# Loads of running sums behind their units' weights, running sums later, delta rule a block later

## The chip, the core and the metric

The kernel runs on one core of a Trainium2 chip. The core has five engines that work side by side, each through its own queue in order: PE (TensorE, matrix products), DVE (VectorE), ACT (ScalarE, functions and copies), POOL (GpSimd) and SP (SyncE), whose queue issues most of the transfers. The metric is the device time of one execution in microseconds (us); lower is better. Of several timed runs the median counts. One further execution was recorded by the hardware profiler, and all statements about single instructions come from it.

## What is computed

All data is float32. The input is `x`, 16 sequences of 128 tokens with 256 features. Three parts follow each other:

```python
x = x + delta_rule(attention(x, cond_1))        # attention and gated delta rule
x = x + quantized_ffn(lora_ffn(x, itok_B_0_7))  # two feed-forward parts
```

The attention has 16 heads of 16 features, a causal mask, and a factor per sequence on the scores. Its output feeds the gated delta rule, of which the part around this change is

```python
g = -exp(A_log) * softplus(h @ W_a + dt_bias)      # logarithms of the decays, 32 heads
g = cumsum(g within chunks of 64 tokens)           # the running sums
decay = tril(exp(g[:, None] - g[None, :]))
A = tril(-(k_beta @ k.T) * decay, -1);  T = inverse(I - A)
u = T @ v_beta;  w = T @ (k_beta * exp(g))
```

Keys, queries and values come from `h @ W_qkv`, a causal convolution over four tokens and a SiLU; keys and queries are normalised. The outputs of the chunks are normalised, gated and projected, and added to `x`. The feed-forward parts are not touched by the change.

## The kernel before

The 16 sequences are cut into four groups of four (512 tokens). There are two streams of work, which the kernel weaves together in one program order.

**The attention** (`attention()`) works in blocks: one sequence and half of the heads, so 32 blocks, eight to a group. A block multiplies keys with queries (L243 on PE), masks (L248, DVE), takes the largest (L253, DVE), subtracts it (L256, POOL), takes the exponent (L259, ACT), sums and inverts (L263, L264, DVE), multiplies to shares (L267, POOL), turns them (L274 on PE, copied by L275 on ACT), weighs the values (L282, PE) and picks the halves that belong together (L289 on ACT, L290 on DVE). Three buffers `sc` hold the scores of blocks in flight. A group's output steps are two products with the output weights (L306), the logarithms (`logs`, L310 to L334: product L316, functions on ACT, `gd` on DVE at L332) and `running`. This last forms the running sums by three products with triangular matrices (L339, L341), copies them on DVE (L343, L346) and stores them to DRAM as `sums` (L344).

Each step has a due time, in blocks: block number plus an offset inside the block. A group's output steps are due 2.15, 2.45, 3.0 and 3.6 after the group's last block has started its own slot, so that `running` is due 0.6 blocks behind `logs`.

**The delta rule** works in units: one key head (two value heads) and one group, so 64 units, in groups of 16 heads. Slot `n` of the main loop (L857) issues the steps of several units at once: the keys of unit `n`, the decays of unit `n - 1`, the inverse for batches of four units (five and six slots late), values, merging and outputs from seven slots late. Inside a slot each step has a time between 0 and 24.

A unit's keys are two projections (L455, PE), convolutions (L464 ACT, L466 DVE, three shifts each), SiLU (L483), squares (L487), norms (L493 PE, L495 DVE), and the factors on POOL (L500 to L507). Its decays start from the running sums: `load_sums(n)` (L428 to L434) loads for a pair of units, `n` and `n + 1`, the sums as the tile `aT` with two transfers of 512 KB each, repeated on all 128 partitions. Five such buffers exist, so that ten units fit. `fades(n)` then subtracts offsets (L443, POOL), masks (L444, POOL) and takes the exponent of the pair (L448, ACT). A weight follows (L522, POOL), and two sets of products of keys with keys and queries (L530 PE, L534 DVE). The diagonal blocks go through small transfers (L543) to one tile for four units, from which the inverse is formed (L557 to L638, mostly DVE). `load_qk(u)` (L392 to L396) loads the unit's key and query weights `w_qk` in two transfers; there are two buffers.

**How the two are woven.** Attention steps due before `ALONE` run first, alone. The others are dealt out over the slots, `PACE` blocks to a slot:

```python
ALONE, PACE = 11.2, 3.9
...
now = [a for a in ahead if a[0] < ALONE + PACE * (n + 1)]
plan([f for _, _, f in now], [24 * ((t - ALONE) / PACE - n) for t, _, _ in now])
```

With these values the attention is done in slot 6, and the other buffers of the delta rule are opened in slot 7.

**What sets the order on an engine.** The kernel is written in a framework that records the instructions in program order with their dependencies, then orders each engine's queue itself: earlier program order has priority, but an instruction that its model of the machine takes to be ready may pass one that is not. So a transfer whose buffer is free can be moved far ahead of its place in the program. This holds for `load_sums`, which the main loop calls at the end of every odd slot and which at first finds all five buffers free. `tc.issue_after(ins)` adds an order to this: what is issued inside it on the engine of `ins` stays behind `ins` in the queue. It adds no wait for completion.

Of the kernel before, what the change touches and what calls it, by code (L numbers as in the profile page):

```python
# [15 lines left out]
P = 128  # L16
# [14 lines left out]
KEY = NK * P  # L31
# [25 lines left out]
def tile_adaln_attn_ffn(  # L57
# [8 lines left out]
    nc = tc.nc  # L66
# [81 lines left out]
    GB = GS * ND  # L148

    def attention():  # L150
# [144 lines left out]
        def output(g):  # L295


            d = {}

            def product(e):  # L300
                if e == 0:
                    hTs[g] = keep.tile([P, ND, GT], F32, name="hT", tag="hT", bufs=2) if g < 2 else \
                        p1.tile([P, ND, GT], F32, name="hT_out", tag="hT_out", bufs=1)
                ps = ps_b.tile([P, GT], F32, name="ps_h", tag="b")
                for c in range(ND):
                    T.matmul(ps, lhsT=wo_sb[:, c, e * P : (e + 1) * P], rhs=grp[g]["oT"][:, c, :],  # L306
                             start=c == 0, stop=c == ND - 1)
                A.copy(hTs[g][:, e, :], ps)

            def logs():  # L310
                if g > 1:
                    nc.sync.dma_start(out=h_dram[g], in_=hTs[g])
                ps = ps_b.tile([P, GS, 2 * NV], F32, name="ps_ba", tag="b")
                for j in range(GS):
                    for c in range(ND):
                        T.matmul(ps[:, j, :], lhsT=hTs[g][:, c, j * S : (j + 1) * S], rhs=wba[:, c, :],  # L316
                                 start=c == 0, stop=c == ND - 1)
                a = p1.tile([P, GS, NV], F32, name="a", tag="ga", bufs=1)
                e = p1.tile([P, GS, NV], F32, name="ea", tag="ge", bufs=1)

                A.activation(e, ps[:, :, 0:NV], AF.Exp, scale=-1.0)
                V.tensor_tensor(a, ps[:, :, NV:], dtb[:, None, :].to_broadcast([P, GS, NV]), ALU.add)
                V.tensor_scalar(e, e, 1.0, None, ALU.add)
                V.reciprocal(beta[:, :, g * GS : (g + 1) * GS, :].rearrange("p k b h -> p b k h"),
                             e.rearrange("p b (k h) -> p b k h", h=2))

                V.scalar_tensor_tensor(out=e, in0=a, scalar=-1.0, in1=a, op0=ALU.mult, op1=ALU.max)
                A.activation(e, e, AF.Exp, scale=-1.0)
                A.activation(e, e, AF.Ln, bias=one)
                V.scalar_tensor_tensor(out=a, in0=a, scalar=0.0, in1=e, op0=ALU.max, op1=ALU.add)  # L330
                gd = d["gd"] = p1.tile([P, NK, GS, 2], F32, name="gd", tag="gd", bufs=1)
                V.tensor_tensor(gd.rearrange("p k b h -> p b k h"), a.rearrange("p b (k h) -> p b k h", h=2),  # L332
                                nega.rearrange("p (k h) -> p k h", h=2)[:, None, :, :].to_broadcast([P, GS, NK, 2]),
                                ALU.mult)  # L334

            def running():
                gd = d["gd"].rearrange("p k b h -> p (k b h)")
                ps = ps_b.tile([P, 3, NK * NP], F32, name="ps_sums", tag="b")
                T.matmul(ps[:, 0, :], lhsT=gd, rhs=tri, start=True, stop=True)  # L339
                for i, w in enumerate((tri, tri_2)):  # L340
                    T.matmul(ps[:, 1 + i, :], lhsT=w, rhs=gd, start=True, stop=True)  # L341
                rows = p1.tile([P, S], F32, name="rows", tag="ge", bufs=1)
                V.tensor_copy(rows, ps[:, 0, :])  # L343
                nc.sync.dma_start(out=sums[g], in_=rows)  # L344
                for i in range(2):
                    V.tensor_copy(off[:, :, g * GS : (g + 1) * GS, :, i].rearrange("p k b h -> p k (b h)"),  # L346
                                  ps[:, 1 + i, :].rearrange("p (k q) -> p k q", k=NK))

            return [lambda: product(0), lambda: product(1), logs, running]
# [3 lines left out]
        def plan(t0, fs, times):  # L353
            steps.extend((t0 + t, len(steps) + i, f) for i, (t, f) in enumerate(zip(times, fs, strict=True)))

        for g in range(NG):
            t0 = GB * g
            plan(t0, project(g), [-2, -1.8, -1, -0.8, -0.6, -0.4] if g == 0 else [-6.55, -5.55, -4.55, -3.55, -2.85, -1.85])
            for i in range(GS):
                for e in range(ND):  # L360
                    plan(t0 + ND * i + e, block(g, i, e), [0, 0.15, 0.3, 0.45, 0.5, 1.0, 1.05, 1.45, 2.2, 2.45, 2.6, 2.8])
            plan(t0 + GB, output(g), [2.15, 2.45, 3.0, 3.6])
        return sorted(steps, key=lambda t: t[:2])


# [23 lines left out]
    qkv = w_qkv.rearrange("(c p) f -> p c f", p=P)  # L389
    w_qk, w_v, w_gate, w_o, x_in, sum_of, un, batch = {}, {}, {}, {}, {}, {}, {}, {}  # L390

    def load_qk(u):  # L392
        kh, g = u
        w = w_qk[u] = w2.tile([P, ND, 2, P], F32, name="w_qk", tag="wqk")
        nc.sync.dma_start(out=w[:, :, 0, :], in_=qkv[:, :, kh * P : (kh + 1) * P])
        nc.sync.dma_start(out=w[:, :, 1, :], in_=qkv[:, :, KEY + kh * P : KEY + (kh + 1) * P])  # L396

    def load_v(u):
        kh, g = u
# [24 lines left out]
    def load_h(g):  # L424
        hTs[g] = keep.tile([P, ND, GT], F32, name="hT", tag="hT", bufs=2)
        nc.sync.dma_start(out=hTs[g], in_=h_dram[g])

    def load_sums(n):  # L428

        t = sum_of[n] = pc.tile([P, 2, NP, S], F32, name="aT", tag="aT", bufs=5)  # L430
        for i in range(2):
            kh, g = units[n + i]
            nc.sync.dma_start(out=t[:, i].rearrange("p q t -> p (q t)"),
                              in_=sums[g][kh * NP : (kh + 1) * NP].rearrange("q t -> (q t)").partition_broadcast(P))  # L434
# [410 lines left out]
    MERGE, OUT, LAST = 7, 8, 10  # L845
    N = len(units)

    ALONE, PACE = 11.2, 3.9
    load_qk(units[0])
    ahead = attention()  # L850
    while ahead and ahead[0][0] < ALONE:
        ahead.pop(0)[2]()
    for n in range(N + LAST):
        at = lambda lag: units[n - lag] if 0 <= n - lag < N else None
        slot = []

        def plan(steps, times):
            slot.extend((t, len(slot) + i, f) for i, (t, f) in enumerate(zip(times, steps, strict=True)))  # L860

        def spread(steps, t0=0.0, t1=24.0):
            plan(steps, [t0 + (t1 - t0) * (i + 0.5) / len(steps) for i in range(len(steps))])

        now = [a for a in ahead if a[0] < ALONE + PACE * (n + 1)]
        plan([f for _, _, f in now], [24 * ((t - ALONE) / PACE - n) for t, _, _ in now])
        del ahead[: len(now)]
        if n == 0:
            plan([lambda: load_sums(0)], [5])
        if n == MERGE:  # L870
            assert not ahead
            st_1.close()
            open_late()
            load_v(at(MERGE))
        if n + 1 < N:
            load_qk(units[n + 1])
        if at(MERGE - 1) and n >= MERGE:
            load_v(at(MERGE - 1))
        if at(OUT - 1):
            load_z(at(OUT - 1))  # L880
        if at(LAST - 1):
            load_o(at(LAST - 1))
        if n % NK == OUT + 1 and 1 <= n // NK < NG - 1:
            load_h(n // NK + 1)
        if at(MERGE) or at(MERGE + 1):
            steps = mergers(at(MERGE), at(MERGE + 1))
            plan(steps, [0, 0, 8, 14] if at(MERGE) else [14])
        if at(1):
            plan(decays(at(1)), [0, 4.5, 9, 10])
        if at(0):  # L890
            plan(keys(at(0)), [2, 5, 6.0, 10, 12.0, 14, 19])
        if n % 2 == 0 and n < N:
            plan(fades(n), [8, 12, 19])
        if at(MERGE):
            plan(values(at(MERGE)), [5.5, 8.5, 9, 15.5, 18, 23])
        if at(OUT):
            plan(outputs(at(OUT)), [13, 20, 16, 17, 19, 22, 23.5])
        if at(LAST):
            plan(finish_unit(at(LAST)), [0, 8, 14, 14])
        if at(NU + 1) and (n - NU - 1) % NU == 0:  # L900
            first, second = inverse((n - NU - 1) // NU)
            spread(first)
        elif at(NU + 2) and (n - NU - 2) % NU == 0:
            plan(second, [0, 1, 4, 6, 7, 13, 15, 17])
        for _, _, f in sorted(slot, key=lambda t: t[:2]):
            f()
        if n % 2 and n + 1 < N:
            load_sums(n + 1)
        if n == N + 2:
            ffn_loads()  # L910
    late["stack"].close()
# [236 lines left out]
```

## Time and profile before

| | |
|---|---|
| Median of 3 runs | 2430.25 us (2428.03 to 2436.76) |
| The profiled execution | 2431.28 us |
| Its span (first to last instruction) | 2429.6 us |
| PE busy in the span | 2200.7 us, 91% |
| DVE busy | 1548.1 us, 64% |
| ACT busy | 1361.7 us, 56% |
| POOL busy | 1145.9 us, 47% |
| Mean granted TensorE clock | 0.954 |

The profile gives busy time per engine, also in slices and in freely chosen stretches. In a stretch's line stand its bounds and length, then the busy microseconds of PE, of PE's weight loads, of DVE, ACT and POOL, each with its number of instructions, then the granted TensorE clock, the share of the DMA engines and GB/s. A timeline lists instructions by start and length; in brackets stands idle time of the engine just ahead, and which engine and tile ended it. The view of waits adds such idle times up: total, how many, the longest. Tiles are written as output and inputs, `aT<-sums` for example.

### The profile page before, as it was taken

The numbers are of one execution on the slowest core, as the hardware profiler recorded it, in microseconds if no ns is written. First come the engines' busy times: TensorE is split into PE (matmuls) and PEld (weight loads), VectorE is DVE, ScalarE is ACT, GpSimd is POOL, SyncE is SP. The second block draws the span as 40 slices with busy tenths as digits, with TensorE's granted clock in tenths as the row PEclk, the third lists the DMA queues.
The fourth block names the chain that finished last, engine by engine and source line by source line (L and its number), as shares of the span: only waits on it lengthen the run. The fifth ranks groups of instructions, "written<-read, shape, count | busy, mean of one in ns | idle before, by whom it ended". The sixth has DMA issues, their size and how long they took to land. (4 is left out here: it accounts for less than half of the span.)

```text
span 2429.6 us, 41939 instructions
## 1 busy us (share of the span) xinstructions
PE 2200.7 (91%) x16248; PEld 1450.2 (60%) x16248; DVE 1548.1 (64%) x2102; ACT 1361.7 (56%) x3008; POOL 1145.9 (47%) x833
## 2 busy tenths in 40 slices
PE   7868759989999998989999998989999898999999
PEld 3433336766667666766666666766677686344445
DVE  4657878687776968687777868687876831311111
ACT  3566536766666666766666666766666574111110
POOL 4585535465555656465555656465556413700000
PEclk9889879999999999999999999999999999999999
DMA  1200022222222322322223222222322323000000
GB/s 56 91 17 15 24 56 76 70 66 71 68 66 77 104 72 64 75 68 68 68 80 86 82 73 64 77 66 68 85 69 80 89 52 123 26 0 20 9 0 18
DMA packets 289910, 148.37 MB, mean 61 GB/s; under 512 B 184241, under 2 KB 278193, under 8 KB 289713
## 3 DMA queue, kind: packets, MB, share of 16 engines
q1 hardware_dynamic: 287792, 141.44, 21.1%
q0 software_dynamic: 1344, 4.20, 0.5%
q8 instruction: 131, 2.15, 0.4%
q14 instruction: 67, 0.54, 0.1%
q10 hardware_dynamic: 576, 0.05, 0.0%
HBM read 119.13 MB, written 5.51 MB: 51 GB/s over the span
## 5 line engine op out<-in xcount | busy, mean ns | idle before, releaser
L466 DVE SCALAR_TENSOR_TENSOR cv<-ps_in,cw,cv 128x500 f32<-128x500 f32 (+2 forms) x768 | 540.2, 735 | 88.8 <-ACT cv L464 84.2
L455 PE MATMUL ps_in<-hT,w_v 128*128 128x512 f32 x512 | 281.5, 679 | 6.8 <-DVE z L770 4.6
L464 ACT ACTIVATE cv<-ps_in,cw 128x512 f32<-128x512 f32 x256 | 174.5, 682 | 182.7 <-PE ps_in L455 182.0
L770 DVE TENSOR_TENSOR z<-ps_ot,z 128x512 f32<-128x512 f32 x128 | 87.9, 687 | 289.9 <-ACT sq L768 289.9
L455 PE MATMUL ps_in<-hT,w_qk 128*128 128x512 f32 x512 | 251.3, 613 | 7.1 <-DVE z L770 6.2
L743 PE MATMUL ps_z<-w_gate,hT 128*128 128x256 f32 x1024 | 242.3, 379 | 1.7 <-DVE z L770 1.7
L800 PE MATMUL ps_out<-wo_head,zT 128*128 128x256 f32 x1024 | 238.8, 386 | 1.0 <-ACT zT L792 1.0
L500 POOL TENSOR_SCALAR nn<-turned 128x4 f32<-128x4 f32 x64 | 15.6, 244 | 419.4 <-DVE turned L495 316.8
L800 PEld LDWEIGHTS ps_out<-wo_head,zT 128*128 128x128 f32 x1024 | 189.0, 190 | 38.0 <-issue 10.7
L743 PEld LDWEIGHTS ps_z<-w_gate,hT 128*128 128x128 f32 x1024 | 189.4, 190 | 27.7 <-DVE z L770 2.6
L455 PEld LDWEIGHTS ps_in<-hT,w_v 128*128 128x128 f32 x512 | 104.6, 217 | 113.3 <-issue 105.2
L768 ACT ACTIVATE sq<-ps_ot 128x128 f32<-128x128 f32 x512 | 143.2, 280 | 31.6 <-PE ps_ot L762 23.0
L483 ACT ACTIVATE kq<-cv 128x512 f32<-128x512 f32 x128 | 80.1, 626 | 126.8 <-DVE cv L466 126.7
L756 ACT COPY y<-ps_y 128x512 f32<-128x512 f32 x128 | 75.0, 586 | 135.3 <-PE ps_y L755 130.6
L530 PEld LDWEIGHTS ps_kq<-kq 128*128 128x128 f32 x512 | 102.5, 203 | 73.4 <-issue 53.4
L455 PEld LDWEIGHTS ps_in<-hT,w_qk 128*128 128x128 f32 x512 | 94.2, 195 | 84.8 <-issue 67.0
L1055 POOL TENSOR_TENSOR o<-o,x_in 128x512 f32<-128x512 f32 x8 | 10.1, 1265 | 283.4 <-DVE o L1054 283.4
L777 POOL TENSOR_TENSOR z<-z,r 128x1024 f32<-128x1024 f32 x64 | 132.2, 2066 | 23.2 <-DVE z L770 20.4
L790 PE MATMUL ps_zt<-ident,z 128*128 128x128 f32 x512 | 88.9, 301 | 59.4 <-DVE aT L534 57.4
L530 PE MATMUL ps_kq<-kq 128*128 128x256 f32 x512 | 136.8, 391 | 0.0
L762 PE MATMUL ps_ot<-y,aT 128*128 128x128 f32 x1024 | 135.3, 275 | 0.0
L755 PEld LDWEIGHTS ps_y<-v,W 128*128 128x128 f32 x1024 | 123.3, 194 | 16.6 <-ACT W L701 10.8
(212 smaller groups left out, 5004.2 us busy)
## 6 DMA issues: line engine op xcount, KB each, us to landing
aT<-sums SPq DMA_DIRECT2D x64, 512.0 KB, 5.8
w_qk<-in_w_qkv_dram SPq DMA_DIRECT2D x128, 128.0 KB, 2.2
w_v<-in_w_qkv_dram SPq DMA_DIRECT2D x64, 256.0 KB, 2.7
w_gate<-in_w_z_dram SPq DMA_DIRECT2D x64, 256.0 KB, 2.7
wo_head<-in_w_out_dram SPq DMA_DIRECT2D x64, 256.0 KB, 2.7
diag<-bT SPq DMA_DIRECT2D x256, 32.0 KB, 2.0
W<-Uc SPq DMA_DIRECT2D x256, 32.0 KB, 2.0
T<-Tc SPq DMA_DIRECT2D x128, 32.0 KB, 1.9
```

What stands on the lines that cost most here:

```text
L455: T.matmul(ps, lhsT=w[:, c, blk, :], rhs=hTs[g][:, c, :], start=c == 0, stop=c == ND - 1)
L464: A.activation(cv, psv, AF.Copy, scale=cw[:, col, 3:4])
L466: V.scalar_tensor_tensor(out=cv[:, :, sh:], in0=psv[:, :, : S - sh], scalar=cw[:, col, 3 - sh : 4 - sh], in1=cv[:, :, sh:], op0=ALU.mult, ...
L530: T.matmul(ps[:, j, :, :], lhsT=d["kq"][:, s, 0, :], rhs=d["kq"][:, s, :, :], start=True, stop=True)
L743: T.matmul(ps[:, j, :], lhsT=hTs[g][:, c, t0 : t0 + S], rhs=w_gate[u][:, c, :], start=c == 0, stop=c == ND - 1)
L755: T.matmul(ps[:, j, :], lhsT=d["W"][:, p, :], rhs=v[:, p, :], start=True, stop=True)
L762: T.matmul(ps[:, j, :], lhsT=d["aT"][:, p, :], rhs=d["y"][:, p, :], start=True, stop=True)
L768: A.activation(sq, ps[:, j, :], AF.Square, accum_out=d["r"][:, p : p + 1])
L770: V.tensor_tensor(z, ps, z, ALU.mult)
L777: G.tensor_tensor(d["z"], d["z"], d["r"][:, :, None].to_broadcast([P, NP, S]), ALU.mult)
L790: T.transpose(ps[:, j, :], d["z"][:, 4 * n + j, :], ident)
L800: T.matmul(ps[:, j, :], lhsT=d["zT", n][:, 2 * j + h, :], rhs=w_o[u][:, h, :], start=kh == j == h == 0, stop=kh == NK - 1 and j == h == 1)
```

## The change

Three things change. `load_sums` inside the loop is queued behind the last transfer of `load_qk`, which at that point is the load for unit `n + 1`, the first unit of the pair. The last output step of a group, `running`, is due at 4.8 instead of 3.6, thus 1.8 blocks behind `logs`. And `ALONE` and `PACE` go from 11.2 and 3.9 to 12.2 and 3.8: one more block of attention runs alone, and a slot takes in a little less. The first call, `load_sums(0)` in slot 0, stays as it was.

```diff
-            plan(t0 + GB, output(g), [2.15, 2.45, 3.0, 3.6])
+            plan(t0 + GB, output(g), [2.15, 2.45, 3.0, 4.8])
...
+    loads = {}
+
     def load_qk(u):
         kh, g = u
         w = w_qk[u] = w2.tile([P, ND, 2, P], F32, name="w_qk", tag="wqk")
         nc.sync.dma_start(out=w[:, :, 0, :], in_=qkv[:, :, kh * P : (kh + 1) * P])
-        nc.sync.dma_start(out=w[:, :, 1, :], in_=qkv[:, :, KEY + kh * P : KEY + (kh + 1) * P])
+        loads["qk"] = nc.sync.dma_start(out=w[:, :, 1, :], in_=qkv[:, :, KEY + kh * P : KEY + (kh + 1) * P]).ins
...
-    ALONE, PACE = 11.2, 3.9
+    ALONE, PACE = 12.2, 3.8
...
         if n % 2 and n + 1 < N:
-            load_sums(n + 1)
+            with tc.issue_after(loads["qk"]):
+                load_sums(n + 1)
```

Line numbers in this document are those of the kernel before; in the changed kernel lines from L395 on stand two lower down, and three from the end of the main loop on.

## The prediction

> **What bounds the kernel now.** I read the slices of the page first, to see which stretch is slack; then busy time by stretch, the waits of that stretch, and the timelines of four engines. From the page:
>
> ```profile
> PE   7868759989999998989999998989999898999999
> ```
>
> and from busy time by stretch (busy us with instruction counts; clock, DMA share and GB/s last):
>
> ```profile
> 97.00:112.00 15.00, 12.75 (x56) 5.92 (x55) 12.47 (x21) 10.80 (x15) 5.69 (x3) 0.89 0.20 74
> 112.00:158.00 46.00, 25.59 (x104) 13.06 (x103) 19.68 (x30) 25.99 (x37) 45.31 (x32) 0.76 0.26 103
> 158.00:280.00 122.00, 100.88 (x463) 47.11 (x464) 90.70 (x142) 75.58 (x109) 70.76 (x50) 0.92 0.07 17
> 280.00:337.00 57.00, 28.22 (x130) 15.35 (x126) 52.47 (x70) 23.42 (x33) 22.97 (x14) 0.76 0.08 24
> 420.00:2000.00 1580.00, 1471.07 (x13137) 1077.15 (x13136) 1175.98 (x1556) 1063.70 (x2482) 836.06 (x613) 0.97 0.27 73
> ```
>
> The steady part belongs to PE (1471 of 1580 us). The start does not: from 112 to 158 us POOL is full (45.31 of 46) and PE idles 20.4 us; from 280 to 337 us DVE is full (52.47 of 57). The burst at 112 us is visible on the SP queue and on POOL (start, length, instruction):
>
> ```profile
> 103.22 0.34 SPq L344 DMA_DIRECT2D sums<-rows  x1
> 109.16 5.06 SPq L433 DMA_DIRECT2D aT<-sums  x8
> ...
> 121.27 1.90 POOL L256 TENSOR_TENSOR sc<-sc,mx 128x1024 f32<-128x1024 f32 x1
> 123.12 1.90 POOL L267 TENSOR_TENSOR sc<-sc,sm 128x1024 f32<-128x1024 f32 x1
> ...
> 133.38 3.75 POOL L443 TENSOR_TENSOR aT<-aT,off 128x1024 f32<-128x1024 f32 x2
> 137.09 1.89 POOL L267 TENSOR_TENSOR sc<-sc,sm 128x1024 f32<-128x1024 f32 x1
> ```
>
> Sums for five pairs of units arrive together; POOL then runs all ten subtract-and-mask steps (L443, L444), and the softmax steps (L256, L267) queue among them. On PE:
>
> ```profile
> 125.07 1.43 PE L274 MATMUL ps_pt<-ident,sc 128*128 128x128 f32 x8 [3.74 <-POOL sc L267]
> 139.04 1.12 PE L274 MATMUL ps_pt<-ident,sc 128*128 128x128 f32 x4 [9.58 <-POOL sc L267]
> 154.39 1.97 PE L274 MATMUL ps_pt<-ident,sc 128*128 128x128 f32 x8 [4.71 <-POOL sc L267]
> 329.86 0.80 PE L339 MATMUL ps_sums<-tri,gd 128*128 128x128 f32 x2 [20.02 <-DVE gd L332]
> ```
>
> The first three are 18.0 us of PE waiting for POOL. The fourth is the last group's running sums waiting for its logarithms on DVE. The waits of the whole run (total, times, longest) put all four groups' sums together:
>
> ```profile
> PE ps_sums L339 <- DVE gd L332: 26.9, 4, 20.0
> ```
>
> **What the Trainium skill says.** "Perfetto Trace Analysis", section Tensor Engine Instruction, calls ACT, DVE and GPSIMD strict FIFOs: one late POOL step holds all behind it. The trace agrees (the share at 137.09 runs directly behind L443). "GPSIMD Engine Reference", section 1 Specifications, says POOL shares its SBUF interfaces with DVE, with contention for DVE instructions in a 2-port mode or with two SBUF inputs. The trace agrees: L323 on DVE took 4.89 us at 318.57 while a POOL product ran from 317.92 to 323.38, against 0.22 at 248.76.
>
> **The change part by part.** The program order is known and was compared per engine. PE's differs only from the end of the eleventh turned block (96.2 us) to the sums of the last group (331 us); from the key norms of unit 6 on it is the same to the end. So the question is how much earlier PE reaches that point. Later PE is over 93% busy in an unchanged order, so I carry the gain to the end one to one; if the later slack (7%) absorbed some, that part would be lost.
>
> (1) Loads behind weights. Each pair now follows the load of its units' weights, which waits for PE to free a weight buffer. No bytes change. On POOL, four steps stay in the burst (pairs 0 and 1), two go between the norms of units 1 and 2, two between 3 and 4, two after the inverse's products. Six steps move: 6 x (1.93 + 1.12) = 18.3 us (means of L443 and L444 in the groups by line). On SP the six moved issues, about 0.6 us each, now stand among the diagonal stores (2.55 us for four); SP is idle most of this stretch, so the 3.7 us cost nothing unless a diagonal store is needed at once, and the first reader of the diagonals is the inverse at 277.8 us.
>
> (2) Running sums later, units a block later. I walked the four queues from 96 to 160 us in the new order by hand, each step starting at the later of its engine's and its inputs' ends, with durations from the rows of before. Block 11 (counting from 1) is turned before the unit's first projection instead of after it (done at 99.3 against 107.3), and the sums run at 103.6 instead of 100.3, without a wait. The reciprocal of block 13 no longer sits behind steps that wait for the burst: its exponent ends at 108.3 once POOL has subtracted (105.3 to 107.2), its sum and reciprocal at 113.7, its shares at 115.6 (before 125.0). Then POOL stands for the first sums: the store leaves at 110.6 instead of 103.2, weights pass at 111, and with the 5.3 us that the load took before (106.88 issue to 112.15 use) POOL starts at 118. Queued behind it is block 14's subtraction, 121 to 123, as before. From there POOL gets through two pairs instead of five: three more L443 (5.7) and L444 (3.3), two subtractions, unit 0's norm factors (2.4) and block 14's shares bring it to 138.2, where before they ended at 139.0. Then it is free of the burst: block 16's subtraction ends at 140.1, and block 15's shares, after the turned block 14 and block 13's pick on DVE, at 142.6 (before 154.3). Products of blocks 17, 18, 19 start at 141, 150, 155.5 (before 147, 159, 166). Unit 1's first projection ends at 145.4 (before 143.2), its norms at 158.5 (before 163.3). So attention is about 10 us ahead and the units 4.7. DVE is the engine that fills next, so I weigh by DVE time per slot: attention 3.8 blocks x 4.35 us (two masks 1.4, two reductions 2.4, the rest 0.55) = 16.5; a unit six shifts x 0.735, four products x 0.68, a transpose 0.44 = 7.6. (10 x 16.5 + 4.7 x 7.6) / 24.1 = 8.3 us gained.
>
> (3) Group 1's and 2's sums no longer wait: 3.09 + 1.58 = 4.7 us of PE. PE is not full there (83%); bounds 0 and 4.7, I take half, 2.3.
>
> (4) The moved steps return. Pairs 2 and 3 each put 6.1 us on POOL (58% busy there) where no share is waiting, only the next subtraction; 0 to 6.1 each, I take 1 each, 2.0. Both pairs load about two blocks ahead of use, so the SP waits (weights, and between the halves of pair 2 the store of group 1's sums) hide; if that cover is gone, up to 5.3 us each. The exponent on ACT waits with POOL, with copies of turned blocks behind it: in the same bound. Pair 4 falls in the DVE-bound end. There L323 leaves POOL's product, but L327 (two SBUF inputs) now meets it: about 3.7 us lost for 4.7. L330, L332 and a product may each meet a subtraction of 1.9: bounds -1 and +5, I take +1.5.
>
> (5) Group 3's wait of 20.0 us I cost at nothing. In the new order one more step of key products (L530, 1.9 us) runs ahead of it; then PE needs Tc (L633 ends at 337.1), which DVE sets with 52.47 us of work in 57. With a quicker DVE it would be worth the 2.9 us of products and norms that ran behind the wait.
>
> (6) Two fewer table loads on ACT, 2 x 1.28 us, beside a 56% busy engine; two changed orders of SP stores at 335 us, 2.6 us of diagonal issues ahead of the last sums store, six microseconds before w_v is used: nothing, or 1 us if w_v lands late.
>
> Sum: -8.3 - 2.3 + 2.0 + 1.5 = -7.1. The profiled execution took 2431.28 us (span 2429.6, 1.7 outside), 1.0 above the median of 2430.25. So 2424.2 for a like execution and 2423 for the median.
>
> **Rivals.** 0.5% of 2430 is 12.15 us, about what a measurement here can tell from no change: the lines are 2418.1 and 2442.4.
>
> Faster: all 18.0 us of PE waits go and the sums' 4.7 too, the moved steps hide in POOL's 42% slack. For it: at 160 us attention is 10 us ahead, and 158 to 280 us still has 31 us of DVE idle to gain from. Against it: the units start later, and the end needs them. 2430 - 22.7 = 2407.5.
>
> No effect: attention's lead is lost before DVE fills, since the tail must wait for unit work that began later; the units' 4.7 us less 3.5 returned leaves 2429.
>
> Slower: pairs 2 and 3 reach POOL late. Each then costs landing 5.3 + work 6.1 = 11.4 us with softmax queued behind, 22.8 for two, less 8.3: +14.5, 2445. It decides if the load is issued under 5.3 us before POOL gets there. For it: POOL already stood 2.33 us at L443 before the first sums. Against it: the two blocks between.
>
> That loads bunch anyway can be excluded: the new edge is in SP's order.
>
> **How the numbers follow.** My forecast 45% (2416 to 2430), faster rival 27%, no effect 18%, slower 10%. A twentieth of the forecast's own spread lies under 2418. So faster by over 0.5%: 0.32, within: 0.58, slower: 0.10. Range: 2405 leaves some 9% below, inside the faster rival; 2440 leaves the slower rival's 10% above. That also spans (4)'s upper bounds.
>
> **What would show it.** Right: aT loads in twos on SP between 110 and 345 us; POOL under 80% busy and PE's three share waits under 6 us in all from 112 to 158 us; the sums waits of groups 0 to 2 gone; DVE still full before Tc; w_v used near 337 instead of 344 us; after that equal lengths. Wrong: POOL idle before L443 for pairs 2 or 3 by over 3 us (slower), Tc earlier by over 12 us (faster), or a lead at 160 us that is gone at 280.

## The result and the profile after

The changed kernel takes 2433.07 us (median of 20 runs, 2427.93 to 2439.17) against 2428.9 (20 runs) for the kernel before beside it. The ratio is 1.0016, with an interval of 1.0008 to 1.0023: 2 to 6 us slower. That lies within 0.5% and inside the range given, but on the other side of no change than the forecast of 2423. Its profiled execution took 2437.61 us (span 2435.9), 4.5 us above its median, so traces are used below for places and orders, and medians for totals.

Busy time by stretch in the changed kernel (columns as before):

```profile
97.00:112.00 15.00, 10.38 (x46) 4.29 (x40) 10.12 (x15) 7.92 (x12) 5.64 (x3) 1.00 0.02 5
112.00:158.00 46.00, 35.15 (x147) 17.06 (x147) 26.50 (x43) 29.57 (x43) 31.63 (x22) 0.78 0.18 57
158.00:280.00 122.00, 94.43 (x428) 47.52 (x428) 85.58 (x134) 69.50 (x103) 78.83 (x56) 0.87 0.12 34
280.00:337.00 57.00, 29.03 (x130) 14.51 (x126) 50.94 (x68) 25.21 (x34) 26.20 (x15) 0.74 0.14 41
420.00:2000.00 1580.00, 1471.45 (x13126) 1074.97 (x13125) 1179.74 (x1557) 1060.15 (x2477) 839.71 (x614) 0.96 0.28 73
```

The stretch that the change aims at is better by far: from 112 to 158 us POOL falls from 45.31 to 31.63 us of 46, PE rises from 25.59 to 35.15, DVE from 19.68 to 26.50. In the very next stretch the gain is paid back: DVE does 85.58 us of work where it did 90.70, PE 94.43 where it did 100.88. From 97 to 280 us DVE has then done 122.20 us of work against 122.85, so nothing is left of the lead. The long part at the end is the same.

The queues of SP and PE in the changed kernel, and the same sums of PE's waits as before (total, times, longest):

```profile
110.67 0.34 SPq L344 DMA_DIRECT2D sums<-rows  x1
...
112.25 1.78 SPq L435 DMA_DIRECT2D aT<-sums  x4
...
184.14 0.47 SPq L435 DMA_DIRECT2D aT<-sums  x1
188.15 0.33 SPq L344 DMA_DIRECT2D sums<-rows  x1
188.53 0.43 SPq L435 DMA_DIRECT2D aT<-sums  x1
...
252.31 0.93 SPq L435 DMA_DIRECT2D aT<-sums  x2
...
311.55 0.94 SPq L435 DMA_DIRECT2D aT<-sums  x2
```

```profile
137.39 0.69 PE L274 MATMUL ps_pt<-ident,sc 128*128 128x128 f32 x2 [10.57 <-POOL sc L267]
```

```profile
PE ps_pt L274 <- POOL sc L267: 37.1, 11, 10.6
PE ps_sums L339 <- DVE gd L332: 16.3, 1, 16.3
```

Two pairs are loaded at 112 us, the others one at a time; the store of the first sums (110.67) and the first load (112.25) stand where the walk by hand had put them. PE's waits for shares from 112 to 158 us went from 18.0 to 10.6 us, all of it in the one wait shown. The waits of the sums of groups 0 to 2 are gone, that of group 3 went from 20.0 to 16.3. Yet over the whole run PE waits for shares 37.1 us against 40.9: what went at 125 and 154 us came back elsewhere.

Where the lead was lost is read from the ends of the 32 share steps (L267, counted from 1) in both traces. Changed less before: block 15 -10.9 us, block 24 -8.2 (at 220 us), block 25 -5.5 (235), block 26 -2.8 (241), block 27 +1.4 (248), the last one 0.0 (295.5). The units' factors (first POOL step of a unit; units are counted from 0): unit 1 -4.7, unit 2 -3.8, unit 3 +3.2, unit 6 +4.8, unit 7 and on +3.8. The first inverse ends at 339.16 us (Tc) against 337.08. So at 220 us everything was still ahead, and 28 us later nothing was. These timelines of ACT, DVE and PE in the changed kernel show that stretch:

```profile
219.61 1.28 ACT L485 ACT_TABLE_LOAD   x1
220.91 0.63 ACT L485 ACTIVATE kq<-cv 128x512 f32<-128x512 f32 x1
221.44 0.35 ACT L289 ACTIVATE oT<-ps_o,even 128x128 f32<-128x128 f32 x1
223.64 1.07 ACT L275 COPY pT<-ps_pt 128x512 f32<-128x512 f32 x2 [1.85 <-PE ps_pt L274]
225.44 0.37 ACT L289 ACTIVATE oT<-ps_o,even 128x128 f32<-128x128 f32 x1 [0.73 <-PE ps_o L282]
225.71 0.62 ACT L485 ACTIVATE kq<-cv 128x512 f32<-128x512 f32 x1
226.34 1.28 ACT L259 ACT_TABLE_LOAD   x1
227.64 1.06 ACT L259 ACTIVATE sc<-sc 128x1024 f32<-128x1024 f32 x1
228.60 1.04 ACT L489 ACTIVATE sqa<-kq 128x1024 f32<-128x1024 f32 x1
...
228.72 1.22 DVE L263 TENSOR_REDUCE sm<-sc 128x8 f32<-128x1024 f32 x1 [2.97 <-ACT sc L259]
...
229.69 1.08 PE L495 MATMUL ps_n<-sqa,ones 128*32 128x256 f32 x8 [4.30 <-ACT sqa L489]
230.70 2.08 PE L243 MATMUL ps_sc<-ke,qT 64*128 64x512 f32 x4
```

ACT's queue holds here, in this order: the first SiLU of unit 3, a turned block, the second SiLU, the exponent of the next block, the squares. The last input of the second SiLU, a convolution step on DVE, was done at 222.9 us, but the SiLU stood behind the copies of the turned block until 225.71, the exponent behind the SiLU and a change of table until 227.64, and the squares behind that. PE waited 4.30 us for the squares, with the scores of the next block behind; DVE stood still from 225.7 to 228.7. In the kernel before the same three steps have the order SiLU, squares, exponent, and PE waits 0.36 us for the squares:

```profile
226.84 0.63 ACT L483 ACTIVATE kq<-cv 128x512 f32<-128x512 f32 x1 [0.52 <-DVE cv L466]
...
228.44 1.05 ACT L487 ACTIVATE sqa<-kq 128x1024 f32<-128x1024 f32 x1
...
233.19 1.06 ACT L259 ACTIVATE sc<-sc 128x1024 f32<-128x1024 f32 x1
...
229.53 0.64 PE L493 MATMUL ps_n<-sqa,ones 128*32 128x256 f32 x8 [0.36 <-ACT sqa L487]
```

### The profile page after: what moved, and what is told of

It is laid out like the page before. It is cut to its first block, busy times and chain, and to the rows that moved or that the text cites. A ratio compares the mean times of both kernels' runs of the same rounds, so it can differ in the third digit from the quotient of the medians.

```text
span 2435.9 us, 41940 instructions
## 1 busy us (share of the span) xinstructions
PE 2206.4 (91%) x16248; PEld 1453.0 (60%) x16248; DVE 1548.1 (64%) x2102; ACT 1356.9 (56%) x3006; POOL 1145.9 (47%) x833
```

## The experiments

The three edits are called edge (loads behind weights), sums (4.8 for 3.6) and start (12.2 and 3.8 for 11.2 and 3.9). Each ratio is to the kernel before, run beside it. Traces differ by up to 6 us before 90 us, where the queues still hold the same instructions in the same order (in the trace of the edge alone blocks are 5.8 us ahead at 83 us, before the edge acts). So places in traces are compared after taking off what they differ by at 89 us, where the text says nothing else; how much of such an early lead would last to the end is not shown.

**The edge alone.**

```diff
         if n % 2 and n + 1 < N:
-            load_sums(n + 1)
+            with tc.issue_after(loads["qk"]):
+                load_sums(n + 1)
```

> The kernel before with one part alone: loads of running sums queued behind the weights. Theory A (the later start loses the lead, the thinner burst by itself is a gain): the lead of 5 to 10 us at 160 us partly lasts, about 2425 us, 4 below before. Theory B (what leaves the burst comes back: two steps each at 190 and 260 us, and the fifth pair delays unit 6 at the end of the start): about 2433 us, 4 above before, with the norm factors of unit 6 near 339 us instead of 335.

Measured: 2433.47 us, ratio 1.0012 (1.0005 to 1.0019). The edge alone costs about 3 us.

**Without the edge: sums and start.**

```diff
-            with tc.issue_after(loads["qk"]):
-                load_sums(n + 1)
+            load_sums(n + 1)
```

> The changed kernel without the queueing behind the weights; running sums later and the later start stay. Theory A: the loss is the later start's, so 2433 us as the changed kernel, or worse, since the burst is back. Theory B: the loss is the queueing's, so 2429 us or less, with unit 6's factors back at 335 us.

Measured: 2441.49 us, ratio 1.0048 (1.0036 to 1.0061). The burst is back, as busy time by stretch of this kernel shows (POOL is the fifth engine):

```profile
112.00:158.00 46.00, 33.78 (x118) 15.25 (x117) 21.54 (x33) 25.21 (x35) 42.42 (x29) 0.67 0.33 118
```

So in the company of the other two the same edge is worth 8 us, where alone it costs 3. Prices of edits do not add up here.

**The start alone.**

```diff
-    ALONE, PACE = 11.2, 3.9
+    ALONE, PACE = 12.2, 3.8
```

> The kernel before with one part alone: ALONE and PACE at 12.2 and 3.8. Theory A: 2433 us, slower by about 4. Theory B: no change, 2429 us within 2.

Measured: 2438.97 us, ratio 1.0032 (1.0017 to 1.0046): 8 us slower, the largest price of a single edit.

**The fifth pair held back.** In the changed kernel the four POOL steps of the pair that falls into the DVE-bound end are queued behind the factors of unit 6 (`loads["c", 6]` is the last of these).

```diff
+    def held(f):
+        with tc.issue_after(loads["c", 6]):
+            f()
...
+            fs = fades(n)
+            if n == 8:
+                fs = [lambda f=f: held(f) for f in fs[:2]] + fs[2:]
+            plan(fs, [8, 12, 19])
```

> The changed kernel with one edge more: on POOL the subtract-and-mask steps of the fifth pair stay behind the norm factors of unit 6, so that they and their exponent no longer lie between the inverse's products and unit 6's norms. Theory B: unit 6's factors at about 335.5 us instead of 339.8, and the 3.8 us of delay that the changed kernel has from 340 us on shrink to 0 or 1: 2429 us. Theory A: no change beyond 1 us, 2433 us.

Measured: 2433.53 us, ratio 1.0013 (1.0005 to 1.0022), no different from the changed kernel. The factors of unit 6 came at 334.91 us (changed: 339.78), as expected, but those of unit 7 at 358.03 (357.59). The hold moved the delay by one unit.

**The returned work made small.** In the changed kernel the subtraction and mask of pairs 2, 3 and 4 handle one of the eight 128x128 planes of a unit (`q` is their number), so these units' decays are not computed in full.

```diff
-            t4 = t[:, i].rearrange("p q (i c) -> p q i c", i=2)
-            G.tensor_tensor(t4, t4, o[:, :, :, None].to_broadcast([P, NP, 2, C]), ALU.subtract)
-            G.affine_select(out=t[:, i], in_=t[:, i], pattern=[[0, NP], [1, S]], ...
+            t4 = t[:, i].rearrange("p q (i c) -> p q i c", i=2); q = 1 if n in (4, 6, 8) else NP
+            G.tensor_tensor(t4[:, :q], t4[:, :q], o[:, :q, :, None].to_broadcast([P, q, 2, C]), ALU.subtract)
+            G.affine_select(out=t[:, i, :q], in_=t[:, i, :q], pattern=[[0, q], [1, S]], ...
```

> The changed kernel with the subtraction and the mask of pairs 2, 3 and 4 cut to an eighth of their size (128x128 in place of 128x1024; the decays of those pairs are then not computed in full). 16 us of POOL work leave the stretch from 196 to 345 us, instructions and order nearly unchanged. If the work that the edge brings back late is what eats the lead: some 8 us less than the changed kernel, 2425 us, with the factors of units 3 and 6 (lines of nn on POOL) 4 us earlier and the first inverse (Tc) at 334 us or before. If the later start of the units eats it: 2431 to 2434 us, Tc near 338.

Measured: 2434.32 us, ratio 1.0015 (1.0008 to 1.0022), the changed kernel's own ratio. The work that the edge brings back late costs nothing that can be measured; the first theory of this run falls. (ACT's and DVE's order differs from the changed kernel's in some places too, since the framework orders the queues by its model of durations.)

**The burst made small.** The same edit in the kernel before.

> The kernel before with the same cut: subtraction and mask of pairs 2, 3 and 4 an eighth of their size (their decays are then not computed in full), so that most of the burst is gone from 112 to 158 us and nothing comes back later. The best case of what the edge could give. If POOL's burst was worth the 8.3 us that the prediction gave it: 2421 to 2423 us. If slack before 250 us doesn't reach the end: 2428 to 2431, with factors of unit 6 and Tc within 1 us of the kernel before.

Measured: 2430.07 us beside 2430.08, ratio 0.9997 (0.9988 to 1.0006). Its busy time by stretch:

```profile
112.00:158.00 46.00, 27.61 (x125) 13.18 (x123) 23.80 (x37) 29.95 (x41) 34.69 (x33) 0.83 0.28 104
```

POOL fell from 45.31 to 34.69 us, blocks 15 to 24 end 3 to 7 us earlier, the first inverse still 3.5 us. By 626 us all of it is gone. So the burst's work, removed and never returned, is worth nothing at the end, and the lead that it gave went in two parts: some before the first inverse, the rest after it. This is the run that the forecast's main term stands or falls with.

**Edge and sums without the start, and edge and start without the sums.** The first needs the first pair's load and step a little later, since the sums would else be read before they are stored.

```diff
-    ALONE, PACE = 12.2, 3.8
+    ALONE, PACE = 11.2, 3.9
...
-            plan([lambda: load_sums(0)], [5])
+            plan([lambda: load_sums(0)], [10])
...
-            plan(fades(n), [8, 12, 19])
+            plan(fades(n), [8 if n else 10.5, 12, 19])
```

> Edge and later sums, with the units' start as before (11.2 and 3.9); the first pair's load and first step move later by 5 and 2.5 of 24 slot times, since the sums would else be read before they are written. If the later start is what costs (alone it took 8.5 us): 2424 to 2428 us. If the returned POOL work or the later sums cost: 2431 to 2436.

Measured: 2429.4 us, ratio 0.9999 (0.9991 to 1.0008), the time of the kernel before.

```diff
-            plan(t0 + GB, output(g), [2.15, 2.45, 3.0, 4.8])
+            plan(t0 + GB, output(g), [2.15, 2.45, 3.0, 3.6])
```

> Edge and later start, with the running sums where they were (3.6). If the later sums are free or helped by 2 us: 2432 to 2436 us. If they are the part that costs: 2426 to 2429, with the waits of PE for the logarithms back (three of them, 4.7 us).

Measured: 2439.81 us, ratio 1.0036 (1.0022 to 1.005), outside both expectations. So far the start looked guilty: with it, kernels take 2433 to 2441 us, without it 2429 to 2433. The next four runs tested that as a dose.

**One block earlier, and half of the start.** Constants of the four runs, each with the first pair's load and first step placed behind the first sums: edge and sums with 10.2 and 4.0; the kernel before with 10.2 and 4.0; edge and sums with 12.2 and 3.9; edge and sums with 11.2 and 3.8. The last of them, against the changed kernel:

```diff
-    ALONE, PACE = 12.2, 3.8
+    ALONE, PACE = 11.2, 3.8
...
-            plan([lambda: load_sums(0)], [5])
+            plan([lambda: load_sums(0)], [10.5])
...
-            plan(fades(n), [8, 12, 19])
+            plan(fades(n), [8, 12, 19] if n else [11, 12, 19])
```

> Edge and later sums, with the units' start one block the other way: 10.2 and 4.0 (against 11.2 and 3.9 without the change, 12.2 and 3.8 with it; the first pair's load and steps are moved so that they still follow the first running sums). If it is the lateness of the units that sets the end, the dose goes on: less than the run without a later start (2429.4), by up to 4 us, 2425 to 2427, with the factors of units 4 and 6 some 4 us earlier than there. If 11.2 was already the point from which attention sets it: 2430 to 2436.

> The kernel before with the start of 10.2 and 4.0 alone (the first pair's load and steps follow the first running sums). Dose of the start alone: the later start took +8.6. If lateness of the units sets the end: 2422 to 2427. If it is the order in which units and blocks stand in the queues, with no trend: anything from 2427 to 2438.

> The changed kernel with the pace as before: start 12.2, pace 3.9 (changed: 12.2, 3.8; first pair's load and step moved slightly). If the first block's delay is what costs: 2433 to 2436, like the changed kernel, or a little more, since the last blocks now come a whole block later beside the units. If it is the pace: 2429 to 2430.

> The other half: start 11.2 as before, pace 3.8 as changed. If the delay of the start costs: 2428 to 2430, like the run without a later start. If the slower pace of attention beside the units costs: 2433 or more.

Measured, in this order: 2423.55 us, ratio 0.9972 (0.9964 to 0.998); 2430.41, ratio 1.0008 (1.0002 to 1.0014); 2422.57, ratio 0.9977 (0.9968 to 0.9985); 2419.65, ratio 0.9965 (0.9952 to 0.9978). The theory that lateness of the units costs falls with the last two: each half of the start, with edge and sums, gives a kernel faster than the one with neither half (2429.4) and the one with both (2433.07). They differ from the changed kernel in the place of the first pair's load and step too; for 12.2 and 3.9 that move (to 10 and 10.5) was not needed, and no run tells it apart. The run with 11.2 and 3.8 is the fastest kernel of the study. How it differs shows in a stretch where the changed kernel has DVE idle. Busy time by stretch, first of this run, then of the changed kernel:

```profile
240.00:280.00 40.00, 28.84 (x137) 14.12 (x135) 36.86 (x63) 25.70 (x35) 26.12 (x18) 0.87 0.16 45
```

```profile
240.00:280.00 40.00, 26.75 (x126) 13.50 (x126) 27.63 (x45) 20.96 (x31) 26.88 (x19) 0.83 0.14 47
```

DVE works 36.86 of 40 us there against 27.63. In the former the inverse starts at 253.5 us (`lanes<-diag`; changed: 272.4, before: 277.8), in time that DVE else spends idle, and ends at 319.55 us against 339.16 (19.6 earlier, of which 5.0 stood between the two traces already at 89 us). No run isolated this, and it does not explain the other kernel of the two: with 12.2 and 3.9 DVE works 31.93 us of these 40 and the inverse starts at 271.2.

**Moving two instructions.** The place in ACT's queue shown above, taken away: in the changed kernel the second SiLU and the squares of unit 3 go ahead of one block's turned copies and the next block's exponent. Some 15 rows of PE, DVE, ACT and POOL each change places, all within this stretch.

```diff
-            plan(keys(at(0)), [2, 5, 6.0, 10, 12.0, 14, 19])
+            plan(keys(at(0)), [2, 5, 6.0, 6.1, 6.2, 14, 19] if n == 3 else [2, 5, 6.0, 10, 12.0, 14, 19])
...
-            A.activation(d["sqa"], d["kq"], AF.Square)
+            loads["square", index[u]] = A.activation(d["sqa"], d["kq"], AF.Square).ins
...
-                A.activation(d["s"], d["s"], AF.Exp)
+                with tc.issue_after(loads["square", 3]) if (g, i, e) == (3, 0, 0) else ExitStack(): A.activation(d["s"], d["s"], AF.Exp)
...
-                A.copy(d["pT"][:, n], ps)
+                with tc.issue_after(loads["square", 3]) if (g, i, e) == (2, 3, 1) else ExitStack(): A.copy(d["pT"][:, n], ps)
```

> The changed kernel with two ACT instructions of the fourth unit (its second SiLU and its squares) ahead of the turned copies of one block and the exponent of the next, at 223 us; about 15 rows of each queue differ from the changed kernel, all between 220 and 245 us. If this spot loses the lead: PE's wait of 4.3 us for the squares gone, factors of that unit at 230 us (changed: 235.3), and what is kept to the end between 2428 and 2430 us. If the lead is lost anyway further on: 2432 to 2434 us.

Measured: 2429.89 us, ratio 0.9999 (0.9991 to 1.0007), apart from the changed kernel's 1.0008 to 1.0023. ACT and PE in this run (which is 5.8 us ahead from 83 us on):

```profile
218.13 0.64 ACT L485 ACTIVATE kq<-cv 128x512 f32<-128x512 f32 x1 [1.22 <-DVE cv L468]
218.81 1.06 ACT L489 ACTIVATE sqa<-kq 128x1024 f32<-128x1024 f32 x1
219.88 1.28 ACT L259 ACT_TABLE_LOAD   x1
221.18 1.06 ACT L259 ACTIVATE sc<-sc 128x1024 f32<-128x1024 f32 x1
222.14 1.05 ACT L275 COPY pT<-ps_pt 128x512 f32<-128x512 f32 x2
...
219.92 0.64 PE L495 MATMUL ps_n<-sqa,ones 128*32 128x256 f32 x8 [0.81 <-ACT sqa L489]
```

PE's wait for the squares fell from 4.30 to 0.81 us, and unit 3's factors come 7.9 us earlier. At unit 10's factors (430 us) this trace is 6.5 us ahead of the changed kernel's, of which 0.7 us are left if the early 5.8 are taken off in full. The medians differ by 3.2 us, and the executions' granted clock is 0.951 in the mean for both kernels. By the medians this place is worth most of what the changed kernel lost; the trace does not decide it.

**Only the squares ahead of the exponent.** The same without the last pair of lines. DVE's order around the inverse and the last logarithms changes too.

> The changed kernel with the squares of the fourth unit ahead of one exponent only, at 227 us; beyond that spot DVE's order of the first inverse and the last logarithms differs as well. By the spot alone PE's norms come 2.3 us earlier and one softmax sum 1.1 us later: 2431 to 2433 us. If the order of DVE in the tail weighs more: outside of that, by up to 8 us either way.

Measured: 2434.35 us, ratio 1.0015 (1.0005 to 1.0024). Unit 3's factors gain 4 us, unit 4's lose 4, nothing is left.

**The sums alone**, in the kernel before.

> The kernel before with the later running sums alone (the first pair's load and step follow them). Of the corners measured, the sums took 3 us off the edge (2433.5 to 2429.4), added 2.5 to the later start (2439.0 to 2441.5), and took 6.7 off edge and start (2439.8 to 2433.1). If they have a price of their own: the same sign here, 2423 to 2427. If only the resulting order counts: no sign can be told, 2420 to 2440.

Measured: 2430.48 us, ratio 1.0003 (0.9992 to 1.0014): no price and no gain of their own that can be measured. All corners of the three edits, by ratio (the two with sums and without start also have the first pair's load and step later, as above):

| | without start | with start |
|---|---|---|
| neither | 1 | 1.0032 |
| sums | 1.0003 | 1.0048 |
| edge | 1.0012 | 1.0036 |
| edge and sums | 0.9999 | 1.0016 |

**The same swap elsewhere, and two points between.** The run with edge and start but without the sums has the same rows at that place; the move of the two instructions was made there. And two runs stand between the changed kernel's constants and those of these two faster kernels: 12.2 with 3.85, and 11.7 with 3.8.

> Edge and later start without later sums (2439.8), with the two ACT instructions of the fourth unit moved as in the run e13; the rows that differ are the same ones, and none other. If that place has a cost of its own: 3 to 4 us less, 2436 to 2437 us. If the gain hung on the rest of the changed kernel's order: 2439 to 2441 us.

> The changed kernel with pace 3.85 in place of 3.8. By a trend: half way, 2426 to 2429 us. By the particular order: either near 2422, near 2433, or outside of both.

> The changed kernel with start 11.7 in place of 12.2 (the first pair's load and first step 3 and 2 of 24 slot times later, to follow the first sums). By a trend: half way, 2425 to 2428 us. By the particular order: near 2420, near 2433, or outside of both.

Measured: 2437.19 us, ratio 1.0032 (1.002 to 1.0043); 2432.64, ratio 1.0008 (0.9999 to 1.0017); 2436.17, ratio 1.0029 (1.002 to 1.0039). PE's waits from 210 to 250 us, first without the swap, then with it:

```profile
PE ps_n L495 <- ACT sqa L489: 4.3, 1, 4.3
```

```profile
PE ps_n L495 <- ACT sqa L489: 1.1, 1, 1.1
```

The wait goes here too, but the median falls by 2.6 us where the ratios fall by 0.0004, 1 us, and the intervals overlap. So in this kernel a price of the place is not shown. Of the points between, one lies at the changed kernel's end, the other above both ends: there is no trend in the two constants. The run with 3.85 is also against the reading of DVE's gap: DVE works 32.40 us from 240 to 280 us there, more than with 3.9, whose kernel takes 2422.57 us.

## Why the prediction was right or wrong

**What bounds the kernel** was read rightly as far as it went: the steady part carries a difference on as it stands. Measured in the inverses, at `Tc<-inv,gm`, no run's difference to the kernel before is at 1925 us more than 1.5 us from what it was at 517 us (changed: +3.7 and +4.3; without the edge +13.0 and +13.0; 11.2 with 3.8: -13.5 and -12.8). Over these 19 kernels and the kernel before, the time of unit 10's factors, at 423 to 446 us, correlates with the median at 0.96. Nearly all is decided by then; in the run with the small burst 2 us more are lost from there to 626 us.

**(1)** held: loads in twos (the two of pair 2 around the store of group 1's sums), and no late landing: up to 260 us POOL waits for sums 1.99 us once and 0.72 us once. Of its signs, POOL under 80% busy came true (31.63 of 46 us); share waits under 6 us did not (10.6), though the walk in (2), with block 14's shares at 138.2 (measured 137.3), already left room for that wait.

**(2)** failed, and it is the step that turned the sign. Its walk was right: store of the first sums 110.67 (walk: 110.6), POOL's start on them 117.38 (118), block 13's shares 115.4 (115.6), block 15's 143.4 (142.6), unit 1's norms 159.8 (158.5). Wrong was what followed: weighing the leads at 160 us by DVE time, to "8.3 us gained", and carrying that over the 180 us to Tc. The run with the small burst shows that relief of POOL is worth 0 at the end (0.9988 to 1.0006, or -2.9 to +1.5 us), although it is 3 to 7 us ahead in mid course and still 3.5 at the first inverse. So neither the weighing nor the carrying "one to one" through the later part held. In the changed kernel the lead lasts until 220 us and is lost within 28. One place is named there: the second SiLU of unit 3 stands behind a turned block, and its squares behind an exponent. Moving these two takes the median back to that of the kernel before; in the other kernel that has this place no gain is shown.

**(3)** was mis-sized: the waits of groups 1 and 2 went as said, but the sums alone gave 1.0003 (+0.7 us) against the 2.3 us of gain; the lower bound of 0 that stood beside it was right.

**(4)** was mis-sized the other way: the steps that return cost nothing that can be measured (made small: 1.0015, against 1.0016), not 3.5 us. The tail's collision was forecast rightly in kind and size. Timelines of POOL and DVE in the changed kernel:

```profile
317.16 5.45 POOL L580 TENSOR_TENSOR prod<-inv,gm 128x2048 f32<-128x2048 f32 x1 [10.76 <-DVE gm L627]
...
318.43 4.33 DVE L327 SCALAR_TENSOR_TENSOR ea<-a 128x128 f32<-128x128 f32 x1
```

L323 is back to 0.22 us and L327 lasts 4.33 instead of 0.27, as "GPSIMD Engine Reference", section 1 Specifications, in the Trainium skill lets one expect of an instruction with two SBUF inputs. But removing the pair's work there, or holding it back, moved no time.

**(5)** held: group 3's wait fell by 3.7 us, for nothing. **(6)** isn't told apart from the rest: w_v is first used at 346.7 us, 2.9 later than before, where the forecast had it 7 us earlier; Tc is 2.1 us later too.

**The rivals.** "No effect", at 2429, named the mechanism: the lead is lost before DVE fills. It put the cause into unit work that begins later; the runs with half of the start, 2422.6 and 2419.7, speak against that cause. The slower rival's late landings did not occur. What no rival held is that the start, which alone costs 8 us, acts through the order that it gives to the queues and not as lateness; that is argued from the neighbouring constants, which show no trend. The sign "a lead at 160 us that is gone at 280" had been written down as what would make the forecast wrong, and it is what happened. That the result lies inside the range is owed to the range, which takes in the slower rival too, and not to the sum. (The chances 0.32 and 0.58 count the forecast's twentieth as 0.05; a twentieth of its 45% gives 0.29 and 0.61. Nothing hangs on it.)

**A rival that neither the prediction nor the runs took up: the granted clock.** Up to unit 10's factors every one of the twenty kernels has run between 1773 and 1777 products on PE and 458 instructions on DVE, so that this stretch can be compared as a whole. Busy time by stretch in the kernel before, the changed kernel, the one without the edge, and that with 11.2 and 3.8:

```profile
0.00:432.68 432.68, 326.03 (x1773) 173.71 (x1774) 303.32 (x458) 232.76 (x379) 235.55 (x178) 0.87 0.16 47
0.00:436.44 436.44, 329.17 (x1773) 176.32 (x1774) 303.36 (x458) 229.00 (x377) 235.69 (x177) 0.86 0.17 47
0.00:445.80 445.80, 339.07 (x1773) 180.26 (x1774) 304.58 (x458) 232.18 (x379) 235.51 (x178) 0.84 0.16 46
0.00:418.37 418.37, 317.20 (x1773) 169.67 (x1774) 301.06 (x458) 235.43 (x382) 237.66 (x178) 0.89 0.17 49
```

The changed kernel is 3.8 us later than the kernel before, but PE's idle time is 107.3 us against 106.7: the same products took 3.1 us longer, at a lower granted clock. Without the edge it is 13.1 us later with 106.7 us idle, so all of it stands in longer products. In the fastest kernel products are 8.8 us shorter and idle time 5.5 us less (part of that is its early lead of 5 us). Over the twenty traces this clock correlates with the medians at -0.80. In the executions, the changed kernel's 20 have a clock of 0.951 in the mean, where 187 executions of the kernel before, beside the other runs, have 0.953. In the changed kernel's trace the clock is 0.50 from 229 to 235 us, where PE's wait of 4.30 us ends at 229.69, and the norms take 1.08 us there against 0.64 in the kernel before. Whether an order is slow because the clock falls with it, or the clock falls with what makes the order slow, is not shown: no run changed one without the other.

**What stays open.** Which feature of an order makes it fast is not settled, nor the part that the clock has in it. One place matters by the medians in one kernel, and is not shown to in the other that shares it. Earlier inverse work in DVE's idle time is seen in the fastest kernel, and not in the one at 2422.57 us.

## What to carry to other kernels

When two streams are woven into in-order queues, a lead of one stream at some point is worth only what reaches the place where the bounding engine is full; before pricing it by that engine's time, remove the suspected work outright and see whether the end moves at all. An edit of due times is a new order and not only a cost: here neighbouring constants gave 2419.7, 2422.6, 2429.4, 2433.1 and 2436.2 us with the same work, so try several rather than reason about one, look in the trace for an instruction that was ready early but stood behind another stream's wait, and compare the time that the same products took and their granted clock before looking for the difference in waits. A full engine in a slack stretch (POOL, 45.31 of 46 us) was no bound of the kernel.

## What was not expected of the hardware

Traces differ early by up to 6 us with the same instructions in the same order: block 10's shares, before any edit acts, ended at 83.1 us in the trace of the edge alone and at 89.1 in that of the changed kernel. The granted clock goes with it. From 65 to 90 us, first the changed kernel, then the edge alone:

```profile
65.00:90.00 25.00, 22.27 (x84) 10.15 (x84) 14.77 (x22) 12.14 (x22) 14.35 (x9) 0.80 0.01 1
65.00:90.00 25.00, 21.33 (x112) 10.74 (x113) 16.42 (x28) 11.60 (x22) 16.39 (x9) 1.00 0.00 1
```

In the three traces with 1.00 there (the edge alone, 11.2 with 3.8, the two moved instructions) blocks are 4.8 to 5.8 us ahead of the kernel before at 89 us; in the others, all with 0.80, at most 2.2. A difference of single traces below 6 us says nothing unless this is looked at. Later, from 517 to 1925 us, two traces keep their distance to 1.5 us.
